# Table buffers, background pacing and pauses in a deformable-attention and self-attention kernel

## The chip, the cores and the metric

The kernel runs on one core of one Trainium2 chip. The metric is device time in microseconds of one execution; the reported time is the median of several executions. The profile is one further execution, taken by the hardware profiler.

## The reference

The input `x` is 2 x 512 x 32 x 32 in float32. Layer 0 is a deformable attention block: a grouped 1x1 convolution makes `q`; a 6x6 depthwise convolution with stride 4, GELU, a small projection and tanh make sampling offsets on an 8x8 grid; `x` is sampled bilinearly at these points; `k` and `v` come from the samples. The attention bias is a three-layer perceptron of the distance of each of 1024 queries to each of 64 sampling points, for 16 (image, group) pairs. An output projection and a GELU MLP follow. Layer 1 is self-attention over 1024 tokens.

```python
xn = _bn(x, bn1_g, bn1_b)
q = _gconv1x1(xn, qw)
off = gelu(dwconv6x6_stride4(q) + off_dw_b)
off = tanh(einsum('bchw,oc->bohw', off, off_pw_w)) * 4
kv = _grid_sample(xn, grid(off))
k, v = _gconv1x1(kv, kw), _gconv1x1(kv, vw)
pos = grid_q[:, :, None, :] - grid_kv[:, None, :, :]
bias = sign(pos) * log1p(abs(pos))
bias = relu(bias @ cpb_w1 + cpb_b1)       # 2 -> 128
bias = relu(bias @ cpb_w2 + cpb_b2)       # 128 -> 128
bias = bias @ cpb_w3 + cpb_b3             # 128 -> 1
attn = softmax(q k^T * scale + bias)
x = x + out_w @ (attn v) + out_b
x = x + mlp(bn2(x))
# layer 1: x + Wp softmax((Wq x)^T (Wk x) / sqrt(512)) (Wv x)
```

The second perceptron layer, 128 x 128 for 16 x 1024 x 64 positions, is the bulk of the work.

## The kernel before

**The main loop.** `for s in range(NS)` (line 495) runs 256 steps. A step handles 4 of the 64 sampling points of one of 16 (image, group) pairs against all 1024 queries; 16 steps make a pair, called a group here.

- `st_layer1` (line 387) lets VectorE build `h1`, a 128 x 4096 tile: the first perceptron layer as a saturated sum of two small tables, `ta` (x part) and `tb` (y part). It is called two steps ahead (`st_layer1(s + 2)`), and three `h1` buffers exist.
- `st_layer2` (line 405) is 32 TensorE matmuls in four rounds z = 0 to 3, each into one of three PSUM tiles `ps2`, each emptied by one ScalarE activation, into `rx`, `ua`, `rx`, `ub`. The profile counts each float32 matmul as two records, 64 a step.
- `st_sum` (line 424) adds `rx` to `ua` or `ub` on VectorE, and a GpSimd DMA adds `ub` into `ua`. Every second step `st_layer3` (line 430) contracts the sums on TensorE into `sim`.
- `softmax_steps` (line 457) is a generator called `tail`; it takes one step of the finished group's softmax in each loop step. It works in the steps 18 and 19 modulo 32 for the even groups, and in 2, 3, 5 and 6 modulo 32 for the odd ones (from step 34 on).

**The tables.** Every fourth step `st_tables` (line 364) makes a chunk of tables: at step s = 4(c - 1) those of chunk c, which serve the steps 4c to 4c + 3. SyncE loads the distances from a DRAM scratch `fdr`, spread to 128 partitions, into `fb` (one buffer); ScalarE makes `ta` (line 375) and `tb` (line 383) from it, two buffers each. A new `ta` may be written when the last `h1` that reads the old one is built.

**The background.** The inputs of later groups are made while the loop runs. `CHAINS` splits the work in five: chain 0 serves the groups 0 and 1 and runs before the loop; chain 1 serves groups 2 and 3; chains 2, 3 and 4 each hold two channel blocks (K = 2) and serve groups 4 to 7, 8 to 11 and 12 to 15. `later()` (line 340) is a generator over all of it, and each loop step calls `next(bg, None)` once (line 504). For each chain, `chain(ci)` (line 173) does: load `x` (line 119, SyncE), scale it on ScalarE (line 181) and make `q` on TensorE (line 186); 36 taps of the depthwise convolution on VectorE (lines 213 and 215), 3 a step for K = 2 and 6 a step for K = 1; the sum of three accumulators (line 220) and the GELU on ScalarE (line 222); the projection `po` (line 229), tanh and the grid (lines 239 to 251); then sign(d) log1p(|d|) in alternating VectorE and ScalarE instructions on the tile `fe` (lines 254 to 267), and four DMAs to `fdr` (line 269). `sample(ci)` (line 277) then makes bilinear weights on ScalarE and VectorE, transposes `x` (line 303), samples it by matmul (line 315) and makes `k` and `v` (line 331). `st_tables` must not be called for a chain whose `fdr` is not yet written, and line 436 needs `sample` done before the group's last step.

**What sets the order.** The framework derives every semaphore and orders the instructions of each engine's queue itself at compile time, from the program's order and from what it holds ready; each queue then runs in that fixed order. In the trace TensorE's instructions stand in program order: `po` of the chains 1 to 4, which a count of the yields puts into steps 19, 47, 82 and 117, starts at 198, 423, 705 and 989 us, each at the end of that step.

**After the loop** come the projection and MLP of layer 0 and all of layer 1 (from 2028 us on); the diff doesn't touch them.

Of the kernel before, what the change touches and what calls it, by code (L numbers as in the profile page):

```python
# [8 lines left out]
F32 = mybir.dt.float32  # L9
AF = mybir.ActivationFunctionType  # L10
ALU = mybir.AluOpType
# [3 lines left out]
P = 128  # L15
B, C, H, W = 2, 512, 32, 32
# [5 lines left out]
KT = 16  # L22
# [2 lines left out]
NG = 16  # L25

CHAINS = [[(0, 0)], [(0, 1)], [(0, 2), (0, 3)], [(1, 0), (1, 1)], [(1, 2), (1, 3)]]
TAPS = 3
NF = 16
INV_BN = 1.0 / (1.0 + 1e-5) ** 0.5  # L30
# [17 lines left out]
def conv_seq_kernel(ctx: ExitStack, tc: tile.TileContext, x, kst, cst, vec, wsm, outw, w1, w2, wl, out):  # L48
    nc = tc.nc
# [39 lines left out]
    with tc.tile_pool(name="lp", bufs=2) as lp, tc.tile_pool(name="ph", bufs=1) as ph:  # L89
# [83 lines left out]
        def chain(ci):  # L173
            G = CHAINS[ci]
            K = len(G)
            (b, k0), n = G[0], 128 * K
            xn = xn0 if ci == 0 else load(ci)
            yield
            for i in range(K):
                k = k0 + i  # L180
                nc.scalar.activation(
                    xn[:, i, :], xn[:, i, :], AF.Identity, bias=col("bn1b", k), scale=bns[:, k : k + 1]
                )
                ps = flat("psq")
                for h in range(2):
                    nc.tensor.matmul(
                        ps[:, h * 512 : (h + 1) * 512], wq[:, k * P : (k + 1) * P],
                        xn[:, i, h * 512 : (h + 1) * 512], start=True, stop=True,
                    )
                nc.scalar.copy(qa[:, b, k, :], ps)  # L190
                yield


            qv = qa[:, b, k0 : k0 + K, :].rearrange("p k (y x) -> p k y x", x=W)


            acc = ph.tile([P, 3, K, 8, 8], F32, tag="acc", name="acc")
            taps = sorted(range(KS * KS), key=lambda t: any(a in (0, KS - 1) for a in divmod(t, KS)))
            for m, t in enumerate(taps):
                (y0, y1), (x0, x1) = ((1 if a == 0 else 0, 7 if a == KS - 1 else 8) for a in divmod(t, KS))  # L200
                ky, kx = divmod(t, KS)
                ys = slice(4 * y0 - 1 + ky, 4 * y1 - 4 + ky, 4)
                xs_ = slice(4 * x0 - 1 + kx, 4 * x1 - 4 + kx, 4)
                a = acc[:, m % 3]

                if y1 - y0 == 8:
                    ops = [(qv.rearrange("p k y x -> p (k y) x")[:, ky - 1 : ky - 1 + 32 * K - 3 : 4, xs_],
                            a.rearrange("p k y x -> p (k y) x")[:, :, x0:x1])]
                else:
                    ops = [(qv[:, i, ys, xs_], a[:, i, y0:y1, x0:x1]) for i in range(K)]  # L210
                for src, dst in ops:
                    if m < 3:
                        nc.vector.tensor_scalar(dst, src, col("dww", t), None, ALU.mult)
                    else:
                        nc.vector.scalar_tensor_tensor(dst, src, col("dww", t), dst, ALU.mult, ALU.add)  # L215
                if ci > 0 and m % (2 * TAPS // K) == 2 * TAPS // K - 1:
                    yield
            af = acc.rearrange("p a k y x -> p a (k y x)")
            for i in (1, 2):
                nc.vector.tensor_tensor(af[:, 0], af[:, 0], af[:, i], ALU.add)  # L220
            gof = ph.tile([P, K, J], F32, tag="gof", name="gof")
            nc.scalar.activation(
                gof.rearrange("p k j -> p (k j)"), af[:, 0], AF.Gelu, bias=col("dwb")
            )
            yield
            ps = flat("po")
            for i in range(3):
                for f in range(2):
                    nc.tensor.matmul(
                        ps[:, f * 512 + i * n // 2 : f * 512 + (i + 1) * n // 2],  # L230
                        pw[i][64 * f : 64 * f + 64, :],
                        gof[64 * f : 64 * f + 64].rearrange("p k j -> p (k j)"), start=True, stop=True,
                    )
            yield

            th = ph.tile([P, 3, 2 * K, J], F32, tag="th", name="th")
            thf = th.rearrange("p i g j -> p (i g j)")
            for f in range(2):
                nc.scalar.activation(
                    th.rearrange("p i (f k) j -> p f i (k j)", f=2)[:, f],  # L240
                    ps[:, f * 512 : f * 512 + 3 * n // 2].rearrange("p (i m) -> p i m", i=3), AF.Tanh,
                )
            if ci == 0:

                nc.scalar.activation(hb[:, 9:10], thf[:, 3 * n - 1 : 3 * n], AF.Ln, bias=1.0, scale=0.0)
            for i in range(3):
                nc.vector.scalar_tensor_tensor(
                    th[:, i], th[:, i], 4.0, jg[:, i].unsqueeze(1).to_broadcast([P, 2 * K, J]),
                    ALU.mult, ALU.add,
                )  # L250
            nc.vector.tensor_scalar(thf, thf, 2.0 / 7.0, -1.0, ALU.mult, ALU.add)
            yield

            fe = ph.tile([P, 5, n], F32, tag="fe", name="fe")
            pos, ab, u, ln, er = (fe[0:64, i, :] for i in range(5))
            nc.vector.tensor_scalar(pos, thf[0:64, 2 * n : 3 * n], -1.0, gq[0:64], ALU.mult, ALU.add)
            nc.scalar.activation(ab, pos, AF.Abs)
            nc.vector.tensor_scalar(u, ab, 1.0, None, ALU.add)
            nc.scalar.activation(ln, u, AF.Ln)

            nc.vector.scalar_tensor_tensor(er, u, 1.0, ab, ALU.subtract, ALU.subtract)
            nc.vector.reciprocal(u, u)
            nc.vector.tensor_tensor(er, er, u, ALU.mult)
            nc.vector.tensor_scalar(pos, pos, 0.0, 2.0, ALU.is_ge, ALU.mult)
            yield
            nc.vector.tensor_tensor(ln, ln, er, ALU.subtract)
            nc.vector.scalar_tensor_tensor(ab, pos, 1.0, ln, ALU.subtract, ALU.mult)
            for c in range(4):
                nc.sync.dma_start(
                    out=fdr[ci][:, c, :, :].rearrange("g p j -> p g j"),  # L270
                    in_=ab.rearrange("p (g c j) -> p g c j", c=4, j=KT)[:, :, c, :],
                )
            state[ci] = (xn, th)
            yield


        def sample(ci):
# [3 lines left out]
            gx = th[:, 0:2].rearrange("p i g j -> p (i g j)")  # L281

            nc.vector.tensor_scalar(gx, gx, 1.0, 16.0, ALU.add, ALU.mult)
            hx = ph.tile([P, 2, K, J], F32, tag="hx", name="hx")
            hxf = hx.rearrange("p f k j -> p (f k j)")
            nc.scalar.activation(hxf, th[:, 0].rearrange("p g j -> p (g j)"), AF.Abs, bias=hb[:, 0:1])
# [3 lines left out]
            for i, (b, k) in enumerate(G):  # L290
                g = b * NCH + k
# [72 lines left out]
        def st_tables(c):  # L364
            b, k, f = groups[c // 4]
            ci, kk = chain_of[b, k]
            assert ci in state
            fb = lp.tile([P, 2, W, KT], F32, name="fb", bufs=1)
            nc.sync.dma_start(
                out=fb.rearrange("p a x j -> p (a x j)"),  # L370
                in_=fdr[ci][f * len(CHAINS[ci]) + kk, c % 4].rearrange("p j -> (p j)").partition_broadcast(P),
            )
            ta = lp.tile([P, KT, W], F32, name="ta", bufs=2)
            tb = lp.tile([P, KT // 4, H, 4], F32, name="tb", bufs=2)
            nc.scalar.activation(  # L375
                ta.rearrange("p j x -> p x j"), fb[:, 0], AF.Identity, bias=col("cb1"), scale=col("w1x")
            )
            tbv, fbv = tb.rearrange("p i y t -> p y i t"), fb[:, 1].rearrange("p y (i t) -> p y i t", t=4)
            if c == 0:
                nc.vector.tensor_scalar(tbv, fbv, col("w1y"), None, ALU.mult)  # L380
                wake(fb[:, 0].rearrange("p x j -> p (x j)"), 2)
            else:
                nc.scalar.activation(tbv, fbv, AF.Copy, scale=col("w1y"))
            tabs[c] = (ta, tb)
# [106 lines left out]
        bg = later()  # L491
# [3 lines left out]
        for s in range(NS):  # L495
            if s > 0:
                st_sum(s - 1, 2)
            if s % 4 == 0 and s // 4 + 1 < 4 * NG:
                st_tables(s // 4 + 1)
            if s + 2 < NS:  # L500
                st_layer1(s + 2)
            st_layer2(s)
            st_sum(s, 0)
            next(bg, None)
            if tail is not None:
                tail = tail if next(tail, 0) is None else None
            if s % 2 == 1 and s >= 3:
                st_layer3(s - 3)
                if (s - 2) % NSL == NSL - 1:
                    tail = softmax_steps(s // NSL - 1)  # L510
# [282 lines left out]
```

## Time and profile before

| what | value |
|---|---|
| median of 4 runs | 2915.09 us (2914.65 to 2915.24) |
| the profiled execution's own time | 2915.15 us |
| its span, first to last instruction | 2913.4 us |
| mean granted TensorE clock | 0.993 |
| VectorE, ScalarE, GpSimd busy | 1985.2, 1483.9, 235.5 us |
| first matmul of loop step 0, of step 135, of step 255 | 38.9, 1126.3, 2018.6 us |
| background work in the loop ends | about 1135 us (step 135) |

The span leaves 1.75 us of the execution's own time outside of it. A "busy" TensorE counts each matmul from its start to a modelled end, so that short pauses between matmuls are partly hidden; pauses are read from the idle times shown in the timeline. In the timeline a line is a run of equal instructions: start, length, engine, source line, operation, operands, count, and in brackets the idle time before it and what ended it.

### The profile page before, as it was taken

The numbers are of one execution on the slowest core, as the hardware profiler recorded it, in microseconds if no ns is written. First come the engines' busy times: TensorE is split into PE (matmuls) and PEld (weight loads), VectorE is DVE, ScalarE is ACT, GpSimd is POOL, SyncE is SP. The second block draws the span as 40 slices with busy tenths as digits, with TensorE's granted clock in tenths as the row PEclk, the third lists the DMA queues.
The fourth block names the chain that finished last, engine by engine and source line by source line (L and its number), as shares of the span: only waits on it lengthen the run. The fifth ranks groups of instructions, "written<-read, shape, count | busy, mean of one in ns | idle before, by whom it ended". The sixth has DMA issues, their size and how long they took to land.

```text
span 2913.4 us, 46056 instructions
## 1 busy us (share of the span) xinstructions
PE 2861.8 (98%) x20310; PEld 1014.8 (35%) x20310; DVE 1985.2 (68%) x1333; ACT 1483.9 (51%) x1506; POOL 235.5 (8%) x338
## 2 busy tenths in 40 slices
PE   6999999999999999999999999999999999999999
PEld 1333223322332233333333333333444444454444
DVE  6899999899989998999999999997110100013031
ACT  4677677667766776666667676765101001010010
POOL 2111011101101111111111111110000000000000
PEclk8999999999999999999999999999999999999999
DMA  2434344434433443444444444344300100000000
GB/s 86 94 81 103 75 85 93 91 78 83 95 89 74 87 93 79 85 95 88 95 86 90 88 90 92 81 87 95 137 0 0 58 0 0 0 0 4 26 1 29
DMA packets 60584, 197.51 MB, mean 68 GB/s; under 512 B 10592, under 2 KB 11104, under 8 KB 59232
## 3 DMA queue, kind: packets, MB, share of 16 engines
q0 software_dynamic: 36576, 133.19, 23.4%
q1 hardware_dynamic: 22944, 60.30, 7.0%
q8 instruction: 160, 2.62, 0.4%
q10 hardware_dynamic: 864, 1.07, 0.1%
q14 instruction: 40, 0.33, 0.0%
HBM read 56.91 MB, written 4.46 MB: 21 GB/s over the span
## 4 chain that ended last, share of the span: by engine, by line
PE 88%; DVE 7%; ACT 2%; issue 2%; DMA 1%; SPq 0%; ACTq 0%; DVEq 0%
PE ps L412 52%; PE psm L571 8%; PE psh L563 8%; PE pss L643 4%; PE psa L693 4%; PE sim L449 3%; DVE h L395 3%; PE psp L632 2%; PE pso L543 2%; PE psv L682 2%; DVE acc L215 1%; DVE ub L426 1%; PE psg L608 1%; DVE ua L426 1%; PE pkv L315 1%
## 5 line engine op out<-in xcount | busy, mean ns | idle before, releaser
L412 PE MATMUL ps<-h,cw 128*32 128x512 f32 x16384 | 1794.2, 593 | 17.2 <-ACT rx L418 13.7
L395 DVE CUSTOM_DVE_ANT_1 h<-ta,tb 128x4096 f32<-128x4096 f32 (+1 forms) x257 | 1132.3, 4407 | 77.7 <-PE ps L412 73.4
L412 PEld LDWEIGHTS ps<-h,cw 128*32 128x32 f32 x16384 | 528.4, 110 | 1247.8 <-issue 1171.3
L418 ACT ACTIVATE rx<-ps,sc 128x1024 f32<-128x1024 f32 x512 | 569.2, 1112 | 298.7 <-PE ps L412 295.0
L420 ACT ACTIVATE ua<-ps,sc 128x1024 f32<-128x1024 f32 x256 | 307.7, 1202 | 132.0 <-PE ps L412 132.0
L426 DVE SCALAR_TENSOR_TENSOR ua<-rx,sc,ua 128x1024 f32<-128x1024 f32 x256 | 328.2, 1282 | 50.8 <-ACT ua L420 50.5
L428 POOL DMA_DIRECT2D ua<-ub x254 | 218.7, 861 | 1743.9 <-DVE ub L426 1608.0
L420 ACT ACTIVATE ub<-ps,sc 128x1024 f32<-128x1024 f32 x256 | 307.6, 1201 | 100.2 <-PE ps L412 100.2
L426 DVE SCALAR_TENSOR_TENSOR ub<-rx,sc,ub 128x1024 f32<-128x1024 f32 x256 | 327.9, 1281 | 5.6 <-ACT ub L420 5.6
L575 DVE SCALAR_TENSOR_TENSOR xs<-psm,vs,xs 128x512 f32<-128x512 f32 x16 | 12.0, 751 | 425.7 <-PE psm L571 425.7
L567 ACT ACTIVATE hm<-psh,vs 128x512 f32<-128x512 f32 x64 | 44.0, 687 | 364.0 <-PE psh L563 364.0
L571 PE MATMUL psm<-hm,w_s 128*128 128x512 f32 x512 | 220.4, 592 | 0.0
L563 PE MATMUL psh<-xn,w_s 128*128 128x512 f32 x512 | 220.4, 592 | 0.0
L563 PEld LDWEIGHTS psh<-xn,w_s 128*128 128x128 f32 x512 | 97.5, 190 | 122.3 <-issue 122.3
L571 PEld LDWEIGHTS psm<-hm,w_s 128*128 128x128 f32 x512 | 97.4, 190 | 122.3 <-issue 122.3
L449 PE MATMUL sim<-ua,w3s 128*32 128x512 f32 x1024 | 134.7, 596 | 0.0
L643 PE MATMUL pss<-xs,qs 128*128 128x512 f32 x256 | 112.2, 593 | 0.0
L693 PE MATMUL psa<-aT,vt 128*128 128x512 f32 x256 | 110.2, 592 | 0.0
L375 ACT ACTIVATE ta<-fb,vs 128x512 f32<-128x512 f32 x64 | 88.4, 1381 | 38.6 <-DVE h L395 32.6
L649 DVE TENSOR_REDUCE mx<-pss 128x1 f32<-128x1024 f32 x16 | 19.6, 1225 | 118.2 <-PE pss L643 118.2
L636 ACT ACTIVATE qs<-psp,ub 128x512 f32<-128x512 f32 x16 | 11.0, 687 | 137.8 <-PE psp L632 137.8
L698 DVE SCALAR_TENSOR_TENSOR res<-psa,ub,xs 128x512 f32<-128x512 f32 x16 | 12.0, 751 | 97.3 <-PE psa L693 97.3
(138 smaller groups left out, 1069.1 us busy)
## 6 DMA issues: line engine op xcount, KB each, us to landing
ua<-ub POOLq DMA_DIRECT2D x254, 512.0 KB, 4.4
fb<-fdr SPq DMA_DIRECT2D x64, 512.0 KB, 4.8
w_s<-in_w SPq DMA_DIRECT2D x8, 1024.0 KB, 10.4
xn<-in_x SPq DMA_DIRECT2D x8, 512.0 KB, 5.0
xs<-in_x SPq DMA_DIRECT2D x16, 256.0 KB, 8.3
wl_s<-in_wl SPq DMA_DIRECT2D x4, 1024.0 KB, 7.9
out<-res SPq DMA_DIRECT2D x16, 256.0 KB, 2.0
vp<-in_outw SPq DMA_DIRECT2D x1, 1024.0 KB, 7.7
```

Of the source, the lines that this page charges most:

```text
L375: nc.scalar.activation(ta.rearrange("p j x -> p x j"), fb[:, 0], AF.Identity, bias=col("cb1"), scale=col("w1x"))
L395: nc.vector._custom_dve(TENSOR_ADD_SAT, out=h1[:, y : y + step].rearrange("p y t x -> p (y t x)"), in0=a.unsqueeze(1).to_broadcast([P, ste ...
L412: nc.tensor.matmul(ps[32 * q : 32 * q + 32, h, :], cw2[:, 32 * z : 32 * z + 32], h1[:, 16 * h : 16 * h + 16, q, :], start=True, stop=True,)
L418: nc.scalar.activation(o, ps, AF.Relu, bias=sc[:, 4 + z : 5 + z])
L420: nc.scalar.activation(o, ps, AF.Relu, bias=sc[:, 4 + z : 5 + z], scale=sc[:, z : z + 1])
L426: nc.vector.scalar_tensor_tensor(r[1], r[0], sc[:, z : z + 1], r[1], ALU.mult, ALU.add)
L428: nc.gpsimd.dma_start(out=sums[s][1], in_=sums[s][3], accum_op=ALU.add)
L449: nc.tensor.matmul(sims[gi][q : q + 32, :], w3s[:, 28 - 4 * i : 60 - 4 * i], sums[s + e][z][:, h, :], start=(i == 0), stop=(i == NSL // 2 ...
L563: nc.tensor.matmul(ps, w1_s[:, k, i * P : (i + 1) * P], xn2[:, k, :], start=(k == 0), stop=(k == NCH - 1),)
L571: nc.tensor.matmul(ps, w2_s[:, i, o * P : (o + 1) * P], hm[:, i, :], start=(i == 0), stop=(i == NF - 1),)
L643: nc.tensor.matmul(ps[:, h, :], qs[:, k, t * P : (t + 1) * P], xs[:, k, b, h * 512 : (h + 1) * 512], start=(k == 0), stop=(k == NCH - 1),)
L693: nc.tensor.matmul(ps, vt[:, m, o * P : (o + 1) * P], aT[:, m, n], start=(m == 0), stop=(m == 7),)
```

## The change

Five edits:

1. `ta` and `tb` get three buffers in place of two; `fe` shrinks from five rows to four, since the row `er` is now kept in `ab` and the result is written to `u`.
2. The loop calls `next(bg, None)` at each step below 76 and from there in two of three steps (s % 3 of 0 and 1).
3. `chain` yields once more between the sum of the accumulators and the GELU, and between `pos` and its absolute value.
4. `sample` yields once more between the scaled grid and its first ScalarE instruction.
5. `chain` yields twice after the load of `x`.

```diff
+FAST = 76
@@ chain
             xn = xn0 if ci == 0 else load(ci)
             yield
+            yield
@@
             for i in (1, 2):
                 nc.vector.tensor_tensor(af[:, 0], af[:, 0], af[:, i], ALU.add)
+            yield
             gof = ph.tile([P, K, J], F32, tag="gof", name="gof")
@@
-            fe = ph.tile([P, 5, n], F32, tag="fe", name="fe")
-            pos, ab, u, ln, er = (fe[0:64, i, :] for i in range(5))
+            fe = ph.tile([P, 4, n], F32, tag="fe", name="fe")
+            pos, ab, u, ln = (fe[0:64, i, :] for i in range(4))
             nc.vector.tensor_scalar(pos, thf[0:64, 2 * n : 3 * n], -1.0, gq[0:64], ALU.mult, ALU.add)
+            yield
             nc.scalar.activation(ab, pos, AF.Abs)
...
-            nc.vector.scalar_tensor_tensor(er, u, 1.0, ab, ALU.subtract, ALU.subtract)
+            nc.vector.scalar_tensor_tensor(ab, u, 1.0, ab, ALU.subtract, ALU.subtract)
             nc.vector.reciprocal(u, u)
-            nc.vector.tensor_tensor(er, er, u, ALU.mult)
+            nc.vector.tensor_tensor(ab, ab, u, ALU.mult)
             nc.vector.tensor_scalar(pos, pos, 0.0, 2.0, ALU.is_ge, ALU.mult)
             yield
-            nc.vector.tensor_tensor(ln, ln, er, ALU.subtract)
-            nc.vector.scalar_tensor_tensor(ab, pos, 1.0, ln, ALU.subtract, ALU.mult)
+            nc.vector.tensor_tensor(ln, ln, ab, ALU.subtract)
+            nc.vector.scalar_tensor_tensor(u, pos, 1.0, ln, ALU.subtract, ALU.mult)
             for c in range(4):
                 nc.sync.dma_start(
                     out=fdr[ci][:, c, :, :].rearrange("g p j -> p g j"),
-                    in_=ab.rearrange("p (g c j) -> p g c j", c=4, j=KT)[:, :, c, :],
+                    in_=u.rearrange("p (g c j) -> p g c j", c=4, j=KT)[:, :, c, :],
                 )
@@ sample
             nc.vector.tensor_scalar(gx, gx, 1.0, 16.0, ALU.add, ALU.mult)
+            yield
             hx = ph.tile([P, 2, K, J], F32, tag="hx", name="hx")
@@ st_tables
-            ta = lp.tile([P, KT, W], F32, name="ta", bufs=2)
-            tb = lp.tile([P, KT // 4, H, 4], F32, name="tb", bufs=2)
+            ta = lp.tile([P, KT, W], F32, name="ta", bufs=3)
+            tb = lp.tile([P, KT // 4, H, 4], F32, name="tb", bufs=3)
@@ the loop
-            next(bg, None)
+
+            if s < FAST or s % 3 < 2:
+                next(bg, None)
```

## The prediction

> **What bounds the kernel now.** I read the page first.
>
> ```profile
> PE 2861.8 (98%) x20310; PEld 1014.8 (35%) x20310; DVE 1985.2 (68%) x1333; ACT 1483.9 (51%) x1506; POOL 235.5 (8%) x338
> ...
> L412 PE MATMUL ps<-h,cw 128*32 128x512 f32 x16384 | 1794.2, 593 | 17.2 <-ACT rx L418 13.7
> L395 DVE CUSTOM_DVE_ANT_1 h<-ta,tb 128x4096 f32<-128x4096 f32 (+1 forms) x257 | 1132.3, 4407 | 77.7 <-PE ps L412 73.4
> ```
>
> TensorE is the bound, and the change takes no matmul away. All that can be won is TensorE's idle time while the background runs. So next the busy times of two stretches of the loop, with background (39 to 1134 us) and without.
>
> ```profile
> 39.00:1134.00 1095.00, 1074.63 (x9795) 336.32 (x9796) 1026.37 (x697) 774.43 (x798) 117.77 (x142) 1.00 0.41 87
> 1134.00:2025.00 891.00, 891.00 (x8266) 271.36 (x8268) 826.33 (x393) 610.97 (x558) 102.35 (x119) 1.00 0.43 87
> ```
>
> The first numbers are length and TensorE busy: 20.4 us idle in the first, none in the second. Then who waited in the first stretch, for TensorE and for ScalarE.
>
> ```profile
> PE ps L412 <- ACT rx L418: 13.7, 9, 3.0
> PE pb L483 <- DVE sx L475: 3.2, 1, 3.2
> PE ps L412 <- ACT ub L420: 2.8, 3, 1.3
> ```
>
> ```profile
> ACT ta L375 <- DVE h L395: 32.6, 20, 5.4
> ACT xn L181 <- DMA xn<-in_x: 7.7, 4, 5.0
> ACT gof L222 <- DVE acc L220: 6.0, 2, 3.5
> ...
> ACT fe L257 <- DVE fe L256: 4.3, 3, 1.7
> ```
>
> TensorE waits for a PSUM tile that ScalarE has not emptied, and ScalarE stands behind a table, an `x` load, a GELU or `fe`. The timeline around 630 us shows how:
>
> ```profile
> 629.13 1.20 ACT L420 ACTIVATE ua<-ps,sc 128x1024 f32<-128x1024 f32 x1 [0.60 <-PE ps L412]
> 630.21 4.47 DVE L395 CUSTOM_DVE_ANT_1 h<-ta,tb 128x4096 f32<-128x4096 f32 x1
> ...
> 634.71 1.28 ACT L375 ACTIVATE ta<-fb,vs 128x512 f32<-128x512 f32 x1 [4.38 <-DVE h L395]
> ...
> 636.38 1.09 ACT L418 ACTIVATE rx<-ps,sc 128x1024 f32<-128x1024 f32 x1
> ...
> 637.53 5.79 PE L412 MATMUL ps<-h,cw 128*32 128x512 f32 x52 [2.46 <-ACT rx L418]
> ```
>
> `ta` sits between the rounds z = 1 and z = 2 of step 73, while the program asks for it in step 76. So ScalarE's queue isn't in program order: `ta` was put where its buffer was held to come free, right behind the `h` that reads the old table (step 73 builds h of step 75). VectorE is late, ScalarE idles 4.38 us and TensorE 2.46: the first 1.9 us are hidden by the PSUM tiles. In the clean stretch `ta` takes the same place with no idle before it: its slack is zero, but nothing is late.
>
> **What makes VectorE late.** Without background a step lasts (2018.6 - 1126.3)/120 = 7.44 us. VectorE needs 6.7 of it (an h starts at 1595.70, the add behind it at 1600.03, the next at 1601.23: 4.33 + 2 x 1.20), so about 0.6 us a step is free, softmax aside. The taps of chain 3 are 12 steps of program (69 to 80), but VectorE runs them from 599 to 654 us, in steps 69 to 76: 13.5 us of work (16 taps 0.36 us apart, 8 of 0.34, 24 halves of 0.21) in 8 steps that have 5 free. They were pulled forward up to six steps into time that isn't there.
>
> **The stock to be won.** Idle by waits: 13.7 + 3.2 + 2.8 + 0.3 (`ua`, a smaller row) = 20.0. Twice the granted clock fell to a half afterwards: 0.55 mean over 930.20 to 933.60 and 0.72 over 344.70 to 348.10, after idles of 3.01 and 3.22 us; with 3.4 us at half speed each, 3.4 in all. Some 14 stalls each hide 0.16 us in the modelled end of a matmul (592 ns long, groups 430 apart): 2. Together about 25 us, so no version can go below 2915.1 - 25 = 2890. By place: 9 at tables, 4 at the GELU (steps 17 and 77), 5 at the softmax collision (344.80, with its clock), 3.5 at the load of chain 4 (832.83), 2.5 at `fe`, the rest small.
>
> **The parts.**
>
> *Third buffer.* No instruction is added. `ta` of chunk c then needs the h of step 4c - 9 instead of 4c - 5. If queues are filled by readiness, `ta` simply moves four steps earlier and again lands right behind an h, in the same place (after z = 1 of a step 1 modulo 4), with the same wait: 0. If it stays near its program place, the 9 us at tables (with a clock loss up to 11) go. I take 0, because taps were seen six steps ahead of the program, so that four more for `ta` (two and a half now) is near what is shown. Bounds -11 to 0. Behind `ta` on ScalarE stand the PSUM evacuations, and TensorE behind these.
>
> *Thinned steps.* The counts of `next` move, none is added. TensorE's parts stay at their program steps: `q` at 13; 38, 39; 78, 79; 136, 138 (before 11; 32, 33; 67, 68; 102, 103), `po` at 22, 54, 102, 160, the last transposes at 32, 71, 127, the end at 190. But the taps hang on `q` alone, so by the same reading they still run in some 8 steps behind `q`: 0 for the thinning itself, bounds -10 (all lateness of VectorE in tap stages) to +3. What does change is what they meet. Chain 2's taps (40 to 47) no longer meet softmax steps 34 to 38: -5.0. Its place is that of chain 4 before, 64 steps later, so the table stall there (3.0 and its clock) stays in the sum. Chain 3's taps (80 to 87) now meet the softmax of 82 and 83: its VectorE instructions, 0.68 + 0.68 + 0.67 + 0.19 + 0.68 = 2.9 us, all become lateness: +2.9 (0 to 2.9 and a clock loss of 1.7). Chain 1's taps end at 18 to 19, at the softmax of 18 and 19: +1.0 (0 to 2.9). Chain 4's `fe` meets the softmax of 162 and 163 as chain 3's met that of 82 and 83 before: no difference.
>
> *Extra pauses.* GELU and `abs` become program steps later, but ScalarE ran the GELU of step 81 in steps 76 and 77 already; a later place doesn't hold it back: 0, bounds -6.5 (GELU and `fe`) to 0.
>
> *`x` a step earlier.* The scaling ran at 830.5 us, in step 98, as soon as the load landed; the program asked for it in step 102. A pause doesn't move that either. SyncE's queue holds loads of `fb`; the load of `x` started at 822.97, 1.4 us behind one of these, and was waited for 4.99 us; the two that started in steps 27 and 63, away from `fb` loads, were waited for 1.50 and 0.88, which TensorE didn't feel. The new places (behind 32, 71 and 127) are 0 and 3 modulo 4, while `fb` loads follow `tb` in steps 1 modulo 4: -3.2 (-3.5 to 0).
>
> *Late first tables.* Chain 1's `po` moves from 19 to 22, chain 2's from 47 to 54, while their tables are due at 28 and 60 as before. From `po` at 198 us to the landing of the first `fb` took 232.8 + 4.8 - 198 = 39.6 us, 5.4 steps: ready at 27.4 and 59.4, before h needs them (30 and 62), but four or more steps after their buffers are free. So for the first time `ta` waits for a chain of VectorE, two DMAs and ScalarE, guessed by the queue's order: +1.0 (0 to 12.8, as in the third rival).
>
> *Smaller `fe`.* Same instructions, no new wait: 0.
>
> **Sum.** -5.0 + 2.9 + 1.0 - 3.2 + 1.0 = -3.3. Against the profiled execution, 2913.4 of span and 1.75 around it: 2915.15 - 3.3 = 2911.9; against the median 2915.09 the same. I say 2912.
>
> [...] The rows here are 3.01 and 3.22 with the drop, 2.89 (832.83 us) and 2.46 without it. [...]
>
> **Rivals.** (1) Spacing works as the program is written: taps 2 in 3 steps, tables and GELU with slack. For: each edit names one of the four waits. Against: the taps run ahead of their steps. Of 25 us some 5 stay (`q`, projections): 2915 - 20 = 2895. (2) Only the third buffer works: 2912 - 11 = 2901. (3) Slower: the first tables of chains 1 and 2 are placed too early on ScalarE. Each chain has two such waits, since the second load of `fb` also waits for the first `tb`. A wait like the 4.99 us of `x` costs 4.99 - 1.9 = 3.1, about 3.2: 2912 - 1 + 4 x 3.2 = 2924. It decides from a wait of 1.9 us on, and makes the kernel slower from 10 us of TensorE idle in all.
>
> **Chances.** Forecast 0.50 (its own range 2905 to 2920), rival 1 0.20, rival 2 0.12, rival 3 0.18. About 0.2%, 5.8 us, is what a measurement can tell from no change. Faster (below 2909.3): 0.32 of rivals 1 and 2 and a quarter of the forecast's, 0.44. Slower (above 2920.9): three quarters of rival 3 and a little of the forecast's, 0.17. Same 0.39. Range 2894 to 2924: rival 1 to rival 3.
>
> **What would show it.** In the new profile: taps in some 8 steps behind `q`, `ta` still right behind an h and still waiting for it in tap stages (20 us or more in all), no `pb` wait, `x` waits under 2 us, TensorE idle in the stretch about 17 us. Wrong if `ta` no longer waits for h, if the taps spread over 12 or 18 steps, or if `ta` waits for a DMA for over 5 us in steps 25 to 30 or 57 to 62.

## The result, and the profile after

The changed kernel takes **2920.18 us** (median of 35 runs, 2917.33 to 2922.67) against 2915.38 of the kernel before on the same chips (53 runs): ratio **1.0017, 95% interval 1.0012 to 1.0021**. The forecast was 2912. The loss is small, just below the 0.2% that the prediction set for "slower", but its interval leaves no doubt of the sign, and the forecast had the other one.

The profiled execution took 2919.0 us, 2917.2 of it the span. The page after, same groups as shown of before:

```profile
PE 2863.8 (98%) x20310; PEld 1017.7 (35%) x20310; DVE 1984.9 (68%) x1333; ACT 1484.1 (51%) x1507; POOL 235.8 (8%) x338
...
L417 PE MATMUL ps<-h,cw 128*32 128x512 f32 x16384 | 1800.0, 594 | 19.3 <-ACT rx L423 12.3
L400 DVE CUSTOM_DVE_ANT_1 h<-ta,tb 128x4096 f32<-128x4096 f32 (+1 forms) x257 | 1131.4, 4403 | 77.8 <-PE ps L417 73.9
```

No work is added. The same two stretches as before, with length and TensorE busy first:

```profile
39.00:1134.00 1095.00, 1079.00 (x9852) 339.48 (x9856) 1020.66 (x638) 770.99 (x773) 119.27 (x143) 1.00 0.42 88
1134.00:2025.00 891.00, 885.21 (x8164) 271.40 (x8160) 829.43 (x450) 610.79 (x580) 100.86 (x118) 1.00 0.42 85
```

Idle TensorE time in the first is 16.0 us (20.4 before), in the second 5.8 (0 before): the background now reaches to step 190, and took some of its stalls along. Who waits while it runs, first for TensorE, then for ScalarE:

```profile
PE ps L417 <- ACT rx L423: 12.3, 10, 2.7
PE ps L417 <- ACT ub L425: 4.9, 3, 1.8
PE pb L488 <- DVE sx L480: 2.6, 2, 2.1
```

```profile
ACT ta L380 <- DVE h L400: 35.9, 23, 5.3
ACT ta L380 <- DMA fb<-fdr: 13.3, 6, 4.9
ACT gof L225 <- DVE acc L222: 6.2, 4, 2.7
ACT fe L261 <- DVE fe L259: 4.5, 4, 1.6
...
ACT xn L183 <- DMA xn<-in_x: 3.1, 3, 1.7
```

Four readings. `ta` waits for `h` as before (35.9 us against 32.6), third buffer or not. The load of `x` is hidden (longest wait 1.7 us, 5.0 before). `pb` still waits for a softmax, another one. New is the second line: `ta` waits for the DMA of `fb`, 13.3 us in six waits. The timeline at the first such place, ScalarE and then TensorE:

```profile
261.05 1.28 ACT L380 ACTIVATE ta<-fb,vs 128x512 f32<-128x512 f32 x1 [4.88 <-DMA fb<-fdr]
262.13 1.06 ACT L423 ACTIVATE rx<-ps,sc 128x1024 f32<-128x1024 f32 x1
```

```profile
259.01 1.90 PE L417 MATMUL ps<-h,cw 128*32 128x512 f32 x16
263.25 9.12 PE L417 MATMUL ps<-h,cw 128*32 128x512 f32 x64 [2.35 <-ACT rx L423]
```

This is chunk 8, the first of chain 1's tables, in step 28. ScalarE stands 4.88 us at `ta`; behind it in its queue is the evacuation `rx` (the emptying of a PSUM tile) that TensorE needs. The other new place, at 1350 us, VectorE and then TensorE:

```profile
1346.44 4.37 DVE L400 CUSTOM_DVE_ANT_1 h<-ta,tb 128x4096 f32<-128x4096 f32 x1
1350.73 0.68 DVE L480 TENSOR_TENSOR sx<-sx,sm 128x512 f32<-128x512 f32 x1
```

```profile
1351.47 0.66 PE L488 MATMUL pb<-kp,sx 128*128 128x128 f32 x4 [2.08 <-DVE sx L480]
```

VectorE reaches the last softmax instruction of an odd group one `h` too late, behind instructions of chain 4's `fe` (0.41 us) and of its `sample` (`wt`, 1.22 us); the program asks for `pb` right then. That these are the cause is tested below (chain_4_later).

To compare places, I summed for every loop step what the distance of successive matmul starts exceeds 430 ns by (steps over 0.25 us). Time lost at half clock (stretches in which the trace has TensorE's granted clock at 0.5) is therefore included. Each column is one profiled execution, and two executions of one kernel can differ by some us (2917.33 to 2922.67 for the changed kernel), so differences under 1 us mean little. The last two columns belong to kernels that come below: "VectorE in order" is after_vector_in_order, "best version" both_moved_vector_in_order.

| TensorE idle and half clock, us | before | after | after, VectorE in order | best version |
|---|---|---|---|---|
| chain 1: taps, GELU | 1.5 | 1.2 | 1.7 | 2.1 |
| chain 1: `fe`, first tables | 0.5 | 4.7 | 2.0 | 2.0 |
| chain 2: taps, GELU, softmax | 6.8 | 3.2 | 4.4 | 2.3 |
| chain 2: `fe`, first tables | 1.2 | 4.3 | 5.6 | 2.9 |
| chain 3: taps, GELU | 5.2 | 5.3 | 0.9 | 0.6 |
| chain 3: `fe` | 1.8 | 0.7 | 1.0 | 1.4 |
| chain 4: load of `x` | 3.5 | 0 | 0 | 0 |
| chain 4: taps, GELU | 4.5 | 5.1 | 0 | 0 |
| chain 4: `fe`, softmax | 1.0 | 4.7 | 0.8 | 1.0 |
| all of the loop, small ones too | 34.3 | 37.5 | 25.4 | 20.3 |
| first matmul of step 0 to that of step 255 | 1979.7 | 1985.0 | 1972.5 | 1967.6 |

The loop is 5.3 us longer: 3.2 in these idles, the other 2.1 in distances of up to 430 ns, which I can't assign to places. After the loop 1.7 us come back: a stretch at half clock behind it is 6.8 us long in place of 10.2, work that the diff doesn't touch. 5.3 - 1.7 and 0.2 at the start make the 3.8 by which the spans differ.

### The profile page after: what moved, and what is told of

It reads as the page before. It is cut to its first block, busy times and chain, and to the rows that moved or that the text cites. A ratio compares the mean times of both kernels' runs of the same rounds, so it can differ in the third digit from the quotient of the medians.

```text
span 2917.2 us, 46032 instructions
## 1 busy us (share of the span) xinstructions
PE 2863.8 (98%) x20310; PEld 1017.7 (35%) x20310; DVE 1984.9 (68%) x1333; ACT 1484.1 (51%) x1507; POOL 235.8 (8%) x338
## 4 chain that ended last, share of the span: by engine, by line
PE 84%; DVE 11%; issue 2%; ACT 1%; DMA 1%; SPq 0%; ACTq 0%; DVEq 0%
PE ps L417 48%; PE psm L578 8%; PE psh L570 8%; DVE h L400 5%; PE pss L650 4%; PE psa L700 4%; PE sim L454 3%; PE psp L639 2%; PE pso L550 2%; PE psv L689 2%; DVE acc L217 2%; DVE ub L431 2%; DVE ua L431 1%; PE psg L615 1%; DMA fb<-fdr 1%
## 5 line engine op out<-in xcount | busy, mean ns | idle before, releaser
L380 ACT ACTIVATE ta<-fb,vs 128x512 f32<-128x512 f32 x64 | 88.3, 1379 | 55.2 <-DVE h L400 35.9
```

The lines of the kernel that those rows point to most:

```text
L380: nc.scalar.activation(ta.rearrange("p j x -> p x j"), fb[:, 0], AF.Identity, bias=col("cb1"), scale=col("w1x"))
```

## The experiments

The first four take the change apart. Each kernel's ratio is to the kernel before, timed with it on the same chip.

**third_buffer_only**: the kernel before with edit 1 alone.

```diff
-            ta = lp.tile([P, KT, W], F32, name="ta", bufs=2)
+            ta = lp.tile([P, KT, W], F32, name="ta", bufs=3)
```

> The kernel before with the third table buffer (and the four-row fe) alone. Theory A (each queue is filled by readiness, so a further buffer moves each table four steps ahead and it still stands right behind an h): the time of before, 2915 within 3 us; the tables still wait for h some 20 times, over 28 us in all. Theory B (the buffer gives the tables slack): the waits for h fall under 10 us and the time to 2904 to 2906. Theory C (the third buffer is what makes the change slower): 2919 or more.

Measured 2916.85 us, 1.0004 (0.9995 to 1.0013). `ta` waits for `h` 29.3 us in 17 waits, and the idles stand where they stood, but for a new one of 1.6 us at step 25: the first `ta` of chain 1 now starts at 236.90 us (242.79 before) and waits there 1.10 us for its DMA.

**two_buffers**: the changed kernel with two buffers.

```diff
-            ta = lp.tile([P, KT, W], F32, name="ta", bufs=3)
+            ta = lp.tile([P, KT, W], F32, name="ta", bufs=2)
```

> The changed kernel with two table buffers again. Theory A: 2920 within 3 us, since the first tables of chains 1 and 2 wait for their DMA as before and the other tables for h. Theory B (the third buffer was a gain, hidden by losses elsewhere): 2926 or more. Theory C (it is the loss): 2915 or less.

2917.57, 1.0009 (1.0000 to 1.0018); `ta` waits 35.8 us for `h`, as with three. From both sides the third buffer brings nothing: the table is put four steps earlier and stands behind an `h` again. The medians with three buffers are even 1.4 and 2.6 us above those with two; that is near the edge of what these runs can tell.

**no_thinning**: the changed kernel with a background step in every loop step.

```diff
-            if s < FAST or s % 3 < 2:
-                next(bg, None)
+            next(bg, None)
```

> The changed kernel with a background step in every loop step. Chains 1 and 2 stand where they stand in the changed kernel, chain 3 almost, chain 4 some 20 steps earlier. Theory A (taps run ahead of their steps anyway): the taps of chains 3 and 4 take 8 to 10 steps as in the changed kernel, the waits of tables for h stay over 28 us, the two stalls at the first tables (steps 28 and 60, 7.7 us) stay, chain 4 meets the softmax of an odd group again, and the time is 2918 to 2922. Theory D (thinning spaces VectorE's work): more waits, 2925 or more.

2913.76, 0.9995 (0.9986 to 1.0004): faster than expected. Chain 4's `fe` then falls into the steps 134 to 137, at the end of a softmax, and costs 0.6 us (step 138) in place of 4.7. The two late first tables of the chains 1 and 2 cost 8.4 us in this kernel too (9.0 in the changed one), so the thinning didn't make them. Chain 4's taps, in 8 steps as with the thinning, still cost 4.9. So the thinning gave nothing at the taps and moved a later piece to a bad place.

**no_pauses**: the changed kernel without the extra yields of the edits 3 to 5. They are four, not five as the expectation has it; the diff shows one.

```diff
-            yield
             gof = ph.tile([P, K, J], F32, tag="gof", name="gof")
```

> The changed kernel without its five extra pauses, so that chains 1 and 2 stand where they stood before the change. Theory A: tables wait under 3 us for DMAs (13.3 in the changed kernel) and the stalls at steps 28 and 60 go, -7.7; the collision of chain 2 with the softmax (steps 37, 38 and 42, 6.8) returns in place of 3.2 at steps 46 and 47, +3.6: 2920 - 4 = 2916, between 2912 and 2919. If the pauses give slack as they are written: more waits for GELU and fe than 11 us, 2922 or more.

2912.95, 0.9991 (0.9983 to 1.0000), 7.2 below the changed kernel. The idles at the steps 28 and 60 are gone; 3.1 us at the steps 25, 50 and 53 stand in their place. Two other things moved as well: chain 4's `fe` costs 0.8 us in place of 4.7, and the softmax collision of chain 2 is back (6.9 in place of 3.2). I read the first as "the first tables are due before they are ready". The next kernels were to use that, and to test whether tables are the cause of the stalls at the taps or only where they show. They hold instructions in the program's order: `issue_after` adds an edge that puts an instruction, in its own engine's queue, behind the last evacuation (ScalarE) or the last sum (VectorE) that the program has issued by then.

**after_tables_in_order** and **before_tables_in_order**: only `ta` and `tb` are held.

```diff
-                st_tables(s // 4 + 1)
+                with tc.issue_after(at["act"]):
+                    st_tables(s // 4 + 1)
```

> The changed kernel with ta and tb held at their place in the program, behind the last PSUM evacuation of the step before the one that asks for them; all else as it was. Theory A (a table right behind an h blocks ScalarE): the waits of tables for h and for DMA (35.9 and 13.3 us) fall under 3 us, the stalls at steps 28, 46, 60 and 146 and one of those at 85 and 86 go, some 14 of 37 us; what VectorE's lateness does at the GELU and the softmax stays: 2908, between 2903 and 2912. Theory E (TensorE would wait for late h anyway, the table only shows it): 2916 or more, and waits of TensorE for h in place of those for rx.

> The kernel before, with two table buffers, tables held at their place in the program. Theory A: the table's h is then two steps old, so the waits for h (32.6 us) fall under 3 us and the 9 to 11 us at tables go: 2905, between 2902 and 2909. If it needs the third buffer for that: 2912 or more.

2916.74 (1.0005, 0.9996 to 1.0014) and 2914.34 (0.9995, 0.9986 to 1.0003): both miss. The waits of `ta` for `h` vanish, and most of the time doesn't. ScalarE of the first:

```profile
ACT gof L225 <- DVE acc L222: 15.9, 4, 5.2
ACT rx L423 <- DVE ub L433: 8.9, 6, 2.6
```

Before the hold these were 6.2 and 1.7 us. VectorE is as late as ever behind the taps; with the table out of the way, the next thing that needs VectorE takes the wait. `ta` was the messenger there: the idles at the taps of the chains 2, 3 and 4 grow from 3.2, 5.3 and 5.1 to 4.7, 6.6 and 7.2 us.

At the first tables of the chains 1 and 2 it is otherwise: their 9.0 us of idle in the changed kernel are 1.8 here. In step 28 the data come in the same step as in the changed kernel (260.28 against 261.05), but the table stands two evacuations later in ScalarE's queue, waits 1.39 us in place of 4.88, and TensorE runs through:

```profile
260.28 1.41 ACT L380 ACTIVATE ta<-fb,vs 128x512 f32<-128x512 f32 x1 [1.39 <-DMA fb<-fdr]
262.07 1.10 ACT L423 ACTIVATE rx<-ps,sc 128x1024 f32<-128x1024 f32 x1
```

```profile
258.29 13.92 PE L417 MATMUL ps<-h,cw 128*32 128x512 f32 x128
```

Step 60 shows the same (wait 1.79 us, no idle). The hold is the only edit, so it is the table's place in the queue that costs the time there, and not when its data come.

**after_all_in_order** and **before_all_in_order**: the tables and every ScalarE and VectorE instruction of the background are held.

```diff
-                next(bg, None)
+                with tc.issue_after(at["act"]), tc.issue_after(at["dve"]):
+                    next(bg, None)
```

> The changed kernel with tables and all background work of ScalarE and VectorE held at their place in the program, each background step behind the second-last sum and the last evacuation of its loop step. Theory A: taps take 12 to 21 steps, VectorE is never late, stalls of over 1 us vanish but for the first tables of chains 1 and 2, where fe now comes later too: 2900, between 2894 and 2906. Theory E: 2912 or more.

> The kernel before with tables and background held at their place in the program; 3 taps a step in every step. VectorE has 0.6 us a step free and gets 1.1 to 1.3 for 12 steps, so it is late by 6 to 8 us at the end of a chain's taps, within its two steps of lead. Theory A: 2898, between 2893 and 2905. If the thinning to two steps in three is needed: 2908 or more.

2933.74 (1.0061, 1.0049 to 1.0074) and 2921.97 (1.0022, 1.0013 to 1.0032): slower, against expectation. New idles of 3 to 6 us stand at each `q` place (the steps 13, 38 and 39, 78 and 79, 136 and 138 in the first). TensorE waits there for the DMA that adds `ub` into `ua` (11.2 us in five waits) and for the scaling of `x` (3.2 us in two). In after_vector_in_order below, which leaves ScalarE's scaling and its other background work free, none of these steps has over 0.3 us, so ScalarE's running ahead is worth something there. The idles at the first tables grew too (4.8 and 6.9 us at the steps 28 and 60).

**first_tables_early**: the changed kernel, chains 1 and 2 with 8 and 4 taps a step and without the pauses at GELU and `abs`; the steps are given back behind the store to `fdr`.

```diff
-                if ci > 0 and m % (2 * TAPS // K) == 2 * TAPS // K - 1:
+                tps = 8 // K if ci in (1, 2) else 2 * TAPS // K
+                if ci > 0 and m % tps == tps - 1:
                     yield
...
-            yield
+            if ci not in (1, 2):
+                yield
             gof = ph.tile([P, K, J], F32, tag="gof", name="gof")
...
             state[ci] = (xn, th)
             yield
+            for _ in range({1: 4, 2: 5}.get(ci, 0)):
+                yield
```

> The changed kernel with one thing moved: in the chains 1 and 2 the taps take fewer program steps (8 and 4 a step in place of 6 and 3) and the two pauses at the GELU and at abs are left out; the program steps won (4 and 5) are given back behind the store to fdr, so that all later work keeps its program steps. Theory (the loss comes from first tables that are ready too late): the TensorE idle at the steps 28 and 60 (4.3 and 3.4 us, with the one at 57, 0.9) goes, ta no longer waits for a DMA for more than 2 us, everything behind step 61 stays as it was: 2911 to 2914 us against 2920 of the changed kernel. Rival (VectorE's lateness behind the taps stalls ScalarE in any case, at whatever stands next in its queue): the idle comes back as ta waiting for h in the steps 25 or 49 to 53, 2916 to 2920.

**2919.67** (1.0016, 1.0007 to 1.0025): nothing won. The idles left 28 and 60 and came up at 24 and 25 (3.7 and 1.5), 53 and 55 (1.8 and 2.0). My reading of no_pauses falls: it isn't the due time. The same table in this kernel, then in no_pauses, with the evacuation ahead of it or behind it:

```profile
236.75 1.25 ACT L385 ACTIVATE ta<-fb,vs 128x512 f32<-128x512 f32 x1 [2.67 <-DMA fb<-fdr]
237.81 1.16 ACT L430 ACTIVATE ua<-ps,sc 128x1024 f32<-128x1024 f32 x1
```

```profile
234.19 1.19 ACT L421 ACTIVATE ua<-ps,sc 128x1024 f32<-128x1024 f32 x1
235.27 0.39 ACT L297 ACTIVATE wt<-th,hb 128x128 f32<-128x128 f32 x1
236.75 1.37 ACT L376 ACTIVATE ta<-fb,vs 128x512 f32<-128x512 f32 x1 [1.09 <-DMA fb<-fdr]
```

In both the data are there at 236.75. In the first `ua` stands behind the table, in the second ahead of it; the steps 24 and 25 have 5.2 us of idle and half clock in the first and 1.7 in the second. As in after_tables_in_order, what a waiting table costs goes by which evacuation happens to stand behind it. That the queue's order goes by an estimate of when the data are there is my reading; no run tests it.

**chain_4_later**: the changed kernel with four steps more without background, so that chain 4's `fe` comes some six steps later.

```diff
-            if s < FAST or s % 3 < 2:
+            if (s < FAST or s % 3 < 2) and s not in (148, 151, 154, 157):
```

> The changed kernel with four more steps without background (148, 151, 154 and 157), so that chain 4's GELU, projection and fe come four to six steps later and its taps stay where they were. Theory (chain 4's fe made the softmax of the odd group at 162 to 166 late, and its pb transposes with it): the idle at the steps 163, 165 and 166 (0.9, 2.2, 1.6 us, half clock there) goes, the rest stays: 2915 to 2917 against 2920. Rival (the stall belongs to fe and not to what it meets): it moves to the steps 168 to 172, 2919 to 2921.

2915.89 (1.0001, 0.9992 to 1.0010), as expected: the idle of 4.7 us at 163 to 166 is gone and none comes up at the new place of `fe`. The others stand where they stood (the one at 46 loses the clock too, 4.7 us in place of 3.2). So the collision is what cost: 4.3 us by the two medians.

**both_moved**: both of these.

> The changed kernel with both of these: first tables of the chains 1 and 2 early, chain 4's fe later. If the two losses are separate pieces, they add: 2920 - 7.5 - 4.5 = 2908, 2906 to 2910, faster than before by 0.2 to 0.3%. If idle time only moves between messengers, 2914 to 2918.

2915.00 (0.9997, 0.9988 to 1.0006): chain 4's part is there again, the tables' part has nothing to add.

**both_moved_vector_in_order**: both_moved, and held are only VectorE's background, the tables, and the GELU of the chains 2 to 4 (chain 2 has its pause at the GELU again and gives back one step fewer).

```diff
-                st_tables(s // 4 + 1)
+                with tc.issue_after(at["act"]):
+                    st_tables(s // 4 + 1)
...
+                with tc.issue_after(at["dve"]):
+                    next(bg, None)
...
+            with tc.issue_after(at["act"]) if ci > 1 else nullcontext():
+                nc.scalar.activation(
```

> As both_moved, and VectorE's background work, the tables and the GELU of chains 2 to 4 are held at their program places in the queues, while ScalarE's other background work (scaling of x, q) may run ahead as before. Taps then run in 9 steps in chain 2, and in 19 to 24 steps in the chains 3 and 4. Theory (taps pulled together into time that VectorE doesn't have cost 5 us in each of the chains 3 and 4, and holding all of the background failed only by ScalarE's part): no idle at the steps 85 to 89 and 142 to 146, ta waits for h under 5 us in all, 2898 to 2906. Rival (VectorE's lateness reaches the evacuations directly through ub and rx, or the q and projection steps lose their cover): 2910 to 2925.

**2902.33** (0.9954, 0.9942 to 0.9967): the fastest version, 13.2 us below the kernel before. The whole of TensorE's waits while the background runs:

```profile
PE ps L423 <- ACT rx L429: 6.7, 9, 1.5
PE ps L423 <- ACT ub L431: 1.5, 3, 0.6
PE sim L464 <- DMA ua<-ub: 0.9, 2, 0.4
```

They were 21.5 us in the changed kernel; no idle in the loop (the longest of these waits is 1.5 us) halves the clock any more. What the hold does is seen on VectorE in the midst of chain 3's taps (the lines on `acc`), first in the changed kernel, then here:

```profile
703.25 1.40 DVE L217 SCALAR_TENSOR_TENSOR acc<-qa,vs,acc 128x56 f32<-128x56 f32 x6
704.58 1.26 DVE L431 SCALAR_TENSOR_TENSOR ua<-rx,sc,ua 128x1024 f32<-128x1024 f32 x1
705.78 1.97 DVE L217 SCALAR_TENSOR_TENSOR acc<-qa,vs,acc 128x56 f32<-128x56 f32 x7
```

```profile
723.34 1.14 DVE L217 SCALAR_TENSOR_TENSOR acc<-qa,vs,acc 128x128 f32<-128x128 f32 x3
724.37 1.30 DVE L439 SCALAR_TENSOR_TENSOR ub<-rx,sc,ub 128x1024 f32<-128x1024 f32 x1
725.56 4.44 DVE L406 CUSTOM_DVE_ANT_1 h<-ta,tb 128x4096 f32<-128x4096 f32 x1
```

Thirteen tap instructions (halves of taps), 3.4 us, in one step against three (whole taps), 1.1 us. Chain 3's taps run in the steps 80 to 89 there and 81 to 100 here.

The last three ask what of this is the change's own.

**after_vector_in_order**: the changed kernel with this hold, nothing moved. **before_vector_in_order**: the kernel before with it. **vector_in_order_tables_free**: the fastest version without the hold on the tables. The first two carry the three parts of the last diff and no other edit; the third is the last kernel with its first part undone.

> The changed kernel as it is, with the same hold alone: VectorE's background work, the tables and the GELU of the chains 2 to 4 keep their program places in the queues; nothing is moved in the program. Theory (the change spaces the work in the program and the queues undo it; with the order held, its spacing works): no idle above 1.5 us at the steps 80 to 101 and 139 to 166, first tables of the chains 1 and 2 still late by program (fdr in 27 and 59 against tables at 28 and 60), so 4 to 7 us there: 2903 to 2908. Rival (the gain of both_moved_vector_in_order came from the moved places as much as from the hold): 2909 to 2916.

> The kernel before with the same hold and nothing of the change. Its taps are then 3 a step in 12 steps: 13.5 us of work against 7.2 that are free, so VectorE is 6 us late at the end of each of the chains 2 to 4, and the GELU stands directly behind the sum without a pause. Theory (hold and spacing are both needed): GELU waits of 2 to 4 us in the steps 47, 82, 117, 2908 to 2914. Rival (the hold alone does it, the change's spacing is worth nothing even then): 2900 to 2906.

> both_moved_vector_in_order without the hold on the tables: they go into ScalarE's queue where it likes, taps and GELU stay held. Theory (a table is only the first messenger of VectorE's lateness; with the taps spaced, VectorE is late by 2.7 us at most in the chains 3 and 4, so the table costs little there): 2903 to 2908, idle back at tables in the steps 24 to 28, 46 to 60 only. Rival (the hold on the tables is what made the gain): ta waits for h of 20 us or more, 2910 to 2915.

- after_vector_in_order: **2906.75** (0.9970, 0.9959 to 0.9982), as expected. The idles at the taps of the chains 3 and 4 fall from 5.3 and 5.1 to 0.9 and 0.
- before_vector_in_order: **2913.64** (0.9993, 0.9984 to 1.0002), as expected: 12 dense steps of taps leave VectorE late even in order (the GELU waits for it 8.5 us in three waits).
- vector_in_order_tables_free: 2911.74 (0.9986, 0.9977 to 0.9995); in the rival's 2910 to 2915, and `ta` waits for `h` 38.1 us, as the rival said too. The time is therefore the rival's, the places are the theory's. Idle returned where the theory said: 7.8 us at the steps 24 and 25, 4.7 at 46 and 50, 5.9 at 57. At the taps of the chains 3 and 4 it stayed away (1.0 us at step 90 is the largest), though tables are as free there as in the changed kernel:

```profile
ACT ta L386 <- DVE h L406: 38.1, 28, 5.0
ACT ta L386 <- DMA fb<-fdr: 12.7, 3, 6.4
```

`ta` waits for `h` as long as ever in sum, and where the taps are spaced TensorE hardly feels it. The hold on the tables is worth 9.4 us here, most of the gain, and the idles that it takes away stand in the chains 1 and 2; those of the chains 3 and 4 go with the spaced taps. VectorE and the GELU held without the tables gain 3.3 us on both_moved, the tables held alone 3.4 on the changed kernel: the gain takes both.

## Why the prediction went wrong

**The reading of the order held.** Taps ran in 8, 10 and 8 steps behind `q` in the changed kernel whatever the program's spacing; `ta` stood behind an `h` four steps earlier; the pauses held neither GELU nor `abs` back. That the third buffer gains nothing is shown twice. Rival 2, with its 2901, is out. A small slip stands in VectorE's free time: 7.44 - 6.7 is 0.7 us a step, not 0.6; nothing in the sum hangs on it.

**The terms of the sum**, by the table of places:

| term | predicted | measured |
|---|---|---|
| softmax collision of chain 2 | -5.0 | -3.6 |
| chain 3's taps meet the softmax of 82 and 83 | +2.9 | +0.2 |
| chain 1's taps meet that of 18 and 19 | +1.0 | -0.3 |
| chain 4's taps | 0 | +0.5 |
| load of `x` | -3.2 | -3.5 |
| late first tables of chains 1 and 2 (measured with their `fe`) | +1.0 | +7.4 |
| chain 3's `fe` | 0 | -1.2 |
| chain 4's `fe` and the softmax of 162 and 163 | 0 | +3.7 |
| sum | -3.3 | +3.2 |

**The step that failed is the late first tables**, +1.0 in the sum and +7.4 measured. The mechanism was named and bounded (0 to 12.8), and I took a value near the lower end. The argument was that the data are ready at 27.4 and 59.4, before `h` needs them at 30 and 62; the trace has them at 261 us, in step 28, so that part was near. But what decides isn't when `h` needs the table. It is which evacuation stands behind it in ScalarE's queue while it waits: with the table two evacuations later, after_tables_in_order has no idle in the steps 28 and 60. The 4.88 us of the one wait are nearly the 4.99 us of the `x` load that the prediction used for its third rival. The sign that it named for this came, too: about step 28 `ta` waits for its DMA 6.5 us, and about step 60 5.3 us, in two waits each.

That rival's mechanism is what happened, at a smaller price. That its 2924 lies near the measured 2920 is partly luck: it had 12.8 us for the tables, 7.4 came, and 3.7 more came from the slip that follows, which it didn't have.

That moving these tables ahead in the program won nothing (first_tables_early: 9.1 us of idle at them in place of 9.0) fits: the table moves ahead with its data, to the next place where it waits.

**"No difference" for chain 4's `fe` was a slip in reading.** 82 and 83 are 18 and 19 modulo 32, an even group; 162 and 163 are 2 and 3, an odd one, whose softmax goes on to `pb` on TensorE in the steps 165 and 166. The text had both lists and compared them wrongly. The sum had 0 for it, the trace has +3.7, and chain_4_later shows the price by itself: 4.3 us. So the sign "no `pb` wait" failed as well (2.6 us).

**The two softmax terms of the chains 3 and 1** took VectorE's softmax instructions (2.9 us for chain 3, 1.0 for chain 1) as lateness that TensorE feels. By the sums it doesn't: 5.3 us in place of 5.2 and 1.2 in place of 1.5. The two terms above missed by 10.1 us together; the smaller errors, these two chiefly, took 3.6 of that back.

**Rival 1 was the change's intention, and what stood against it is now shown: the order of the queues.** With VectorE's background, the tables and the GELU held, the same program gains 8.8 us on the kernel before (2906.75 against 2915.57), and the same hold without the change 1.9, which is within its uncertainty. The change's spacing and the held order each bring little or nothing alone. "The taps run ahead of their steps" is not the whole of it, since the hold of VectorE and the GELU does little without that of the tables. The 2895 stays out of reach: some 20 us of idle remain in the best version, 9 of them in the chains 1 and 2, whose taps aren't thinned.

**Open.** What holding the GELU adds to the taps and tables wasn't tried alone, nor VectorE's background without the GELU. Nor is it shown what makes up the 2.1 us that the loop lost in distances of up to 430 ns. And no_pauses is 7.2 us below the changed kernel: its first tables cost 5.9 us less and chain 4's `fe` 3.9 less, while the collision of chain 2 costs 3.7 more. That another build would be as lucky with its places isn't shown.

## What to carry to other kernels

Pacing that is written into a program's order can be worth nothing where the framework orders each engine's queue itself: first look in the trace whether the paced instructions run in their steps. If they don't, hold them, but not all: here it paid to hold the engine that is short of time and the few instructions that wait for it on the engine TensorE depends on, while holding the rest of ScalarE's work cost more than was won. A wait in front of a queue may be a messenger: take it away and see whether the time goes too, before pricing it. And price a moved instruction by what stands behind it in its queue, not by when its result is needed.

## What the runs showed of the clock

In every trace with several of them, the stretches at half clock (granted clock 0.5) begin on a fixed grid of 3.413 us: in the changed kernel at 263.89, 1199.14 and 1352.74, which is 274.0 and 45.0 grid steps apart, in the kernel before at 346.18 and 929.86, 171.0 apart. Each of these five lasts one grid step, 3.41 us. Over all 17 traces I summed TensorE's idle time in the loop (distances of matmul starts beyond 430 ns) within each grid step. 37 stretches at half clock began, each right behind a grid step with 2.04 to 3.41 us of idle in it (2.04 and 2.68 in the kernel before; 2.51, 2.71 and 2.14 in the changed one); the grid steps that no half clock followed had up to 2.18. So where a stall lay on the grid mattered: in the changed kernel 2.87 us at step 46 lay across a border (2.12 on the fuller side) and kept the clock, while 2.51 at step 28 (2.35 by the modelled end of the matmul) lay within one grid step and lost it.

The length of a single idle didn't decide. In the kernel before, the idles of 3.01 and 3.22 us that the prediction names had half clock after them, and that of 2.89 us, with 1.96 us in its fuller grid step, had not; in before_tables_in_order one of 3.52 us, ending at 658.81 us, kept the clock, and by the grid it lay half on either side of a border (1.7 and 1.8 us). What of a stall became a clock loss in these runs was thus decided in part by where the grid happened to lie.
